# A graph-transformer network on one core: zero fill, weight loads, weight products and two row sums put in other places

## The chip, the cores and the metric

The kernel runs on one core of a Trainium2 chip. The metric is the device time of one execution in microseconds (us). The core has five engines with a queue of instructions each: PE (TensorE, matrix products), DVE (VectorE), ACT (ScalarE), POOL (GpSimd) and SP (SyncE, which here only issues DMAs). DMAs are issued by SP, ACT and POOL, and are carried out by 16 shared DMA engines.

## The reference, cut to what matters

There are 1250 nodes with 512 channels and 40000 edges with 8 attributes. Two layers follow each other; the change lies in the first.

```python
xn = layernorm(x)
x = x + L0_gnn(xn, edges, edge_attr) + L0_mix(xn)   # both from the same xn
x = x + L0_ffn(layernorm(x))
xn = layernorm(x)
x = x + L1_gnn(xn, edges) + L1_mix(xn)
x = x + L1_ffn(layernorm(x))

def L0_gnn(x, ...):                  # graph transformer
    z = layernorm(x, g, b)
    q, k, v = z @ Wq.T + bq, z @ Wk.T + bk, z @ Wv.T + bv     # 8 heads of 64
    s = (q[src] . k[dst]) / 8 + att_bias                      # per edge and head
    agg = segment_softmax(s, src) summed over v[dst]
    x = x + agg @ Wo.T + bo
    h = silu(layernorm(x, g2, b2) @ W1.T + b1)
    return x + h @ W2.T + b2

def L0_mix(x, ...):                  # linear attention and a small feed-forward
    qp, kp = relu(x @ Wq + bq) + 1e-3, relu(x @ Wk + bk) + 1e-3
    v = x @ Wv + bv
    a = (qp @ (kp.T @ v)) / (qp @ sum(kp))                    # per head
    h = layernorm(a @ Wo + bo + x)
    return layernorm(relu(h @ W1 + b1) @ W2 + b2 + h)

def L1_gnn(x, ...):                  # graph convolution: normalised sums, then two weights
    return (aggregate(x @ W_gcn) + b_gcn) @ W_dense + b_dense
```

## The kernel before, in words

The nodes are padded to 1280, ten tiles of 128. The graph attention is done densely: a DRAM table `adj` of 1280 x 1280 x 9 numbers (eight attribute sums and a count for each pair of nodes, 59 MB) is filled with zeros, the edges are added into it by indirect DMAs, and later each tile of 128 nodes reads its slab of the table.

**Zero fill (lines 219 to 228).** `zrow` is a row of zeros in SBUF, cleared by POOL. Four DMAs of 14.4 MB each, and a small one, write it over `adj`, all issued on SP.

**Edge preparation (to line 293).** From source, target and attributes the kernel makes a key for each edge. Keys are transposed and stored to `key_d` in three DMAs (line 269, on ACT). The weights `wgt` go through an exponential (283) and are split into three bf16 parts in `w3`: three casts and two subtractions on DVE.

**The edge generator `scatter_edges` (line 302 on).** It runs over the 313 columns of 128 edges in batches of three, 105 batches. `load_keys` (311) reads a broadcast row `kr` of keys back from `key_d`. DVE compares keys (`eq` 325, `eqx` 335), TensorE sums the weights of equal keys (317), DVE makes `tot` (342) and `idx` (348), and POOL issues one indirect scatter-add into `adj` for each column (351). `tot` and `idx` have 48 buffers. A scatter waits for those of the batch two before it. A call `pump(n)` in the other code draws n batches from the generator.

**Weight products (`weight_products`, line 402 on).** A second generator multiplies pairs of weights that the later layers need as products: it loads them in halves of 256 columns (`fw`), transposes, multiplies (`product`) and stores to DRAM. It is drawn between the tiles of the mix's attention.

**Stage A (to 799 us).** Under the pool `mix`: x is loaded in ten DMAs on ACT into `xn`, then the weights `wk`, `wv` and the bias rows `mixrows` (lines 456 to 458 by their helpers 129 and 123, on ACT too). Layer norm and transposes for each tile, K and V for each tile (`kp`, `va`, evicted by DVE), the product `kv`, Q, the attention tiles with their layer norm, then the two layers of the mix's feed-forward; its last loop, the f-stage (line 565 on), also adds x and stores to `xm_d`. Under the pool `gqkv` come the graph's layer norm (`z`, line 157), its transposes into `zT` (174), `xb = xn + bo` (stored to `xb_d`), K and Q in column chunks (`kT`, evicted by DVE at 599; `qs` by ACT, stored to `q_d`), V for each tile, and last the gcn fold (lines 613 to 635): `W_gcn @ W_dense` to `wgd_d`, the bias rows to `bsum_d`, and `fold_q`. TensorE's matmuls of all this are recorded at the helper's line 179.

**Slab stage (799 to 1190 us).** `load_tile` (652, 656) loads a slab of `adj` and a tile of `q_d`; the load waits for all scatters.

**The wo stage and the feed-forward (from line 849).** `fetch` loads a tile of the attention's output and of `xb`. Per tile: output projection, sum `X = mm + xb` (884), layer norm (833 to 845), `z` on ACT (889), transposes (897), `zT` (901, 904), and the first feed-forward layer. This loop's order is written out by hand. In the second part the layer's output and `xm` are added to X (921, 922).

**What sets the order.** Except where written by hand, a scheduler chooses the order on each engine when the kernel is built, from modelled times; each engine then runs its queue in order. The DMAs of SP and ACT share eight semaphores, dealt in turn: a DMA which gets a semaphore that an earlier DMA still holds waits on its engine until that one has landed.

Of the kernel before, what the change touches and what calls it, by code (L numbers as in the profile page):

```python
# [22 lines left out]
P = 128  # L23
# [43 lines left out]
def tile_gps_layers(ctx: ExitStack, tc: tile.TileContext, a, out):  # L67
# [13 lines left out]
    def ps_tr(shape=(P, 512), name="tr"):  # L81
        return psum.tile(list(shape), F32, tag="tr", bufs=2, name=name)

# [43 lines left out]
    def load_w(pool, name, kc, n, tag="w", bufs=None, eng=nc.sync):  # L127
        t = pool.tile([P, kc, n], F32, tag=tag, name=name, bufs=bufs)
        eng.dma_start(t, a[name].rearrange("(c p) o -> p c o", p=P))
        return t  # L130
# [65 lines left out]
    adj = dram.tile([NROW, CH], F32, name="adj")  # L196
    key_d = dram.tile([EC, P], F32, name="key_d")
    cnt_d = dram.tile([NP, NP], F32, name="cnt_d")
    q_d = dram.tile([P, KC, NP], F32, name="q_d")
    xm_d = dram.tile([NP, C], F32, name="xm_d")  # L200
    xb_d = dram.tile([NP, C], F32, name="xb_d")
    att_d = dram.tile([P, KC, NP], F32, name="att_d")
    deg_d = dram.tile([P, NP], F32, name="deg_d")
    w1f_d = dram.tile([NEXP, P, KC, 256], F32, name="w1f_d")
    wgd_d = dram.tile([P, KC, C], F32, name="wgd_d")
    wqd_d = dram.tile([P, KC, NKEYS], F32, name="wqd_d")
    bsum_d = dram.tile([P, C], F32, name="bsum_d")

    s_xn = ctx.enter_context(ExitStack())
    pxn = s_xn.enter_context(tc.tile_pool(name="xn", bufs=1, side="right"))
    xn = pxn.tile([P, NT, C], F32, tag="xn", name="xn")

    s_edge = ctx.enter_context(ExitStack())
    pe = s_edge.enter_context(tc.tile_pool(name="edge", bufs=1, side="right"))
    s_tmp = ctx.enter_context(ExitStack())
    ptmp = s_tmp.enter_context(tc.tile_pool(name="edgetmp", bufs=1, side="right"))

    zrow = pe.tile([P, 1800], F32, name="zrow")
    nc.gpsimd.memset(zrow, 0.0)
    adj_p = adj[0:NKEY, :].rearrange("(p r) c -> p (r c)", p=P)
    step = 16 * 1800
    for z0 in range(0, NKEY * CH // P, step):
        nc.sync.dma_start(adj_p[:, z0:z0 + step].rearrange("p (a f) -> p a f", f=1800),
                            zrow[:, None, :].to_broadcast([P, 16, 1800]))
    nc.sync.dma_start(adj[NKEY:NROW, :].rearrange("(p r) c -> p (r c)", p=P), zrow[:, :(G + 1) * CH])
# [74 lines left out]
    def scatter_edges():  # L303
# [3 lines left out]
        def load_keys(c0):  # L307
            cn = min(G + B, EC - c0)
            kr = pew.tile([P, (G + B) * P], F32, name="kr")
            queue = nc.scalar if c0 == 0 else nc.sync  # L310
            queue.dma_start(kr[:, :cn * P],
                            bass.AP(tensor=key_d.tensor, offset=key_d.offset + c0 * P, ap=[[0, P], [1, cn * P]]))
            return kr
# [26 lines left out]
        def scatter(acc, cnt, c0, g, place):  # L340
            tot = pew.tile([P, B, CH], F32, name="tot", bufs=48)
            nc.vector.tensor_reduce(tot[:, :g], acc[:, :g].rearrange("p c (t n) -> p c n t", t=3),
                                    axis=AX.X, op=OP.add)
            row = pew.tile([P, B], F32, name="row")
            nc.vector.scalar_tensor_tensor(row[:, :g], cnt[:, :g], 1.0, keyrel[:, c0:c0 + g],
                                           op0=OP.is_equal, op1=OP.mult)
            idx = pew.tile([P, B], I32, name="idx", bufs=48)
            nc.vector.tensor_tensor(idx[:, :g], row[:, :g], spare[:, place:place + g], op=OP.add)
            near, cur = (scattered[-1] if scattered else []), []
            for c in range(g):  # L350
                st = nc.gpsimd.indirect_dma_start(  # L351
                    out=adj, out_offset=bass.IndirectOffsetOnAxis(ap=idx[:, c:c + 1], axis=0),
                    in_=tot[:, c, :], in_offset=None, compute_op=OP.add)
                for x in cur + near:
                    tc.declare_no_dep(st.ins, x.ins, reason="rows of a batch and of the one next to it differ")
                for x in (scattered[-2] if len(scattered) > 1 else []):
                    tc.add_manual_dep(st.ins, x.ins.name, SYNC, reason="rows of batches may agree")
                cur.append(st)
            scattered.append(cur)
# [40 lines left out]
    def weight_products(pool):  # L400


        def turned(name):
            wT = pool.tile([P, KC, C], F32, tag="fwT", name=name + "T")
            for k in range(KC):
                if k % 2 == 0:
                    w = pool.tile([P, KC, 256], F32, tag="fw", name="fw", bufs=2)
                    nc.sync.dma_start(w, a[name].rearrange("(c p) o -> p c o", p=P)[:, :, k * P:(k + 2) * P])
                ps = ps_tr((P, KC, P))
                for c in range(KC):  # L410
                    nc.tensor.transpose(ps[:, c, :], w[:, c, k % 2 * P:(k % 2 + 1) * P], ident)
                nc.scalar.copy(wT[:, k, :].rearrange("p (c q) -> p c q", c=KC), ps)
            return wT

# [29 lines left out]

    with (tc.tile_pool(name="mix", bufs=1) as pm, tc.tile_pool(name="mixw", bufs=2) as pw,
# [6 lines left out]
        wk = load_w(pm, "L0_mix_Wk", KC, C, bufs=2, eng=nc.scalar)  # L454
        wv = load_w(pm, "L0_mix_Wv", KC, C, bufs=2, eng=nc.scalar)
        rows = rows_bc(pm, a["mix_rows"], len(MIX_ROWS), name="mixrows", eng=nc.scalar)
# [5 lines left out]

        def load_x(t):
            x_t = pw.tile([P, C], F32, tag="x_t", name="x_t")
            if t == NT - 1:
                nc.vector.memset(x_t, 0.0)
                nc.sync.dma_start(x_t[:TAIL], a["x"][t * P:N, :])
            else:
                nc.sync.dma_start(x_t, a["x"][t * P:(t + 1) * P, :])
            return x_t  # L470
# [85 lines left out]
        for t in range(NT):  # L556
            x_t = load_x(t)
# [6 lines left out]
            nc.vector.tensor_tensor(f, f, x_t, op=OP.add)  # L564
# [17 lines left out]
    with tc.tile_pool(name="gqkv", bufs=2) as pq:  # L582
        gbv = rows_bc(pq, a["gnn_rows"][0:2], 2, name="gbv")
# [4 lines left out]
        for t in range(NT):  # L588
            z = pq.tile([P, C], F32, tag="z", name="z")
            norm(pq, z, xn[:, t, :], 1e-5, "lnz")  # L590
            transposed(zT, z, t, "att_g", "att_b")
            xb = pq.tile([P, C], F32, tag="xb", name="xb")
            nc.vector.tensor_tensor(xb, xn[:, t, :], gbv[:, 1, :], op=OP.add)
            nc.scalar.dma_start(xb_d[t * P:(t + 1) * P, :], xb)
        for c0, cn in CHUNKS:
            for m in range(KC):
                ps = ps_mm()
                chan_mm(ps[:, :cn], wk, m, zT, c0, cn)
                nc.vector.tensor_scalar(kT[:, m, c0:c0 + cn], ps[:, :cn], col("gnn_bk", m), None, op0=OP.add)
# [11 lines left out]


        brow = rows_bc(pq, a["l1_rows"], len(L1_ROWS), name="l1rows")
        wg = load_w(pq, "gcn_WgT", KC, C, bufs=3)
        wd = load_w(pq, "L1_gnn_W_dense", KC, C, bufs=3)
        wqn = load_w(pq, "l1_Wq", KC, C, bufs=3)
        for m in range(KC):
            ps = ps_mm()
            mm(ps, [(wg[:, c, m * P:(m + 1) * P], wd[:, c, :]) for c in range(KC)])
            qs = pq.tile([P, 512], F32, tag="qs", name="qs", bufs=3)  # L620
            nc.scalar.copy(qs, ps)
            nc.sync.dma_start(wgd_d[:, m, :], qs)
            pump(1)
        ps = ps_mm()
        mm(ps, [(col("gcn_b", c).to_broadcast([P, P]), wd[:, c, :]) for c in range(KC)])
        qs = pq.tile([P, 512], F32, tag="qs", name="qs", bufs=3)
        nc.vector.tensor_tensor(qs, ps, brow[:, 0, :], op=OP.add)
        nc.vector.tensor_tensor(qs, qs, brow[:, 1, :], op=OP.add)
        nc.sync.dma_start(bsum_d, qs)
        bd = pq.tile([P, KC, H], F32, name="bd")  # L630
        nc.vector.tensor_tensor(bd, own_head, col("l1_wq", 0, 4)[:, :, None].to_broadcast([P, KC, H]), op=OP.mult)
        ps = ps_tr((P, KC, H))
        for m in range(KC):
            mm(ps[:, m, :], [(wqn[:, c, m * P:(m + 1) * P], bd[:, c, :]) for c in range(KC)])
        nc.scalar.copy(fold_q[:, :, :H], ps)
# [212 lines left out]
    with tc.tile_pool(name="gff", bufs=1) as pf, tc.tile_pool(name="gffw", bufs=2) as pw:  # L848

        zT = pf.tile([P, KC, NP], F32, name="zT2")  # L850
        wo = load_w(pf, "gnn_WoT", KC, C)
        inputs, zs = {}, {}
# [8 lines left out]
        def fetch_xm(t):  # L861
            inputs[t] = pw.tile([P, C], F32, tag="xm", name="xm")
            nc.sync.dma_start(inputs[t], xm_d[t * P:(t + 1) * P, :])
# [14 lines left out]
        with tc.manual_schedule(engines={nc.tensor.engine, nc.vector.engine, nc.scalar.engine}):  # L878
            for t in range(NT + 2):
                if t < NT:  # L880
# [3 lines left out]
                    nc.vector.tensor_tensor(X[:, t, :], ps, xb, op=OP.add)  # L884
                    if t + 5 < NT:
                        fetch(t + 5)
# [25 lines left out]
            for c, (c0, cn) in enumerate(CHUNKS):  # L912
                n = cn // P
                for k, t in enumerate(range(c0 // P, c0 // P + n)):
# [7 lines left out]
                    nc.vector.tensor_tensor(X[:, t, :], X[:, t, :], inputs.pop(t), op=OP.add)  # L922
# [1063 lines left out]
```

## Time and profile before

| what | us |
|---|---|
| median of 3 runs | 2408.09 (2406.57 to 2413.21) |
| the profiled execution | 2412.46 |
| its span on the core | 2410.7 |
| last packet of the zero fill | 174.09 |
| slab stage begins, ends | 798.67, 1190 |
| feed-forward's second part ends | 1381 |

Mean TensorE clock granted over the span: 0.913 of full speed. Busy time by stretch, from the trace, in us (columns: stretch, its length, PE, its weight loads, DVE, ACT and POOL with the number of instructions, granted clock, share of the DMA engines, GB/s):

```profile
50.00:80.00 30.00, 0.00 (x0) 0.00 (x0) 13.96 (x7) 5.15 (x5) 0.00 (x0) 1.00 1.02 421
80.00:175.00 95.00, 72.39 (x219) 34.86 (x220) 36.21 (x141) 6.55 (x18) 0.00 (x0) 1.00 1.01 412
520.00:640.00 120.00, 57.51 (x380) 27.88 (x379) 119.52 (x512) 2.43 (x12) 101.11 (x63) 0.60 0.54 111
690.00:772.00 82.00, 80.69 (x369) 42.44 (x368) 47.64 (x207) 5.33 (x9) 68.90 (x44) 1.00 0.46 79
772.00:799.00 27.00, 26.60 (x85) 14.03 (x83) 2.77 (x4) 2.53 (x5) 0.17 (x1) 0.97 0.27 88
```

How to read the rows of the other views. A row of the timeline has start and duration in us, engine, line, operation, output and inputs by the program's names, a count, and in brackets how long the engine idled before it and what released it. Engines with a q are their instruction queues, where DMAs are issued. The chain of waits lists, in order of time, the piece of work that each step waited for. A row of the slices has 40 digits, each the busy share of a fortieth of the span (60 us) in tenths.

### The profile page before, as it was taken

The numbers are of one execution on the slowest core, as the hardware profiler recorded it, in microseconds if no ns is written. First come the engines' busy times: TensorE is split into PE (matmuls) and PEld (weight loads), VectorE is DVE, ScalarE is ACT, GpSimd is POOL, SyncE is SP. The second block draws the span as 40 slices with busy tenths as digits, with TensorE's granted clock in tenths as the row PEclk, the third lists the DMA queues.
The fourth block names the chain that finished last, engine by engine and source line by source line (L and its number), as shares of the span: only waits on it lengthen the run. The fifth ranks groups of instructions, "written<-read, shape, count | busy, mean of one in ns | idle before, by whom it ended". The sixth has DMA issues, their size and how long they took to land.

```text
span 2410.7 us, 29628 instructions
## 1 busy us (share of the span) xinstructions
PE 1986.3 (82%) x10548; PEld 1172.5 (49%) x10548; DVE 1531.4 (64%) x4886; ACT 782.1 (32%) x1465; POOL 695.6 (29%) x448
## 2 busy tenths in 40 slices
PE   0299698675399699999799999999999999978943
PEld 0147465442145366666544545667445446555521
DVE  3528858789892398999550446655222242599997
ACT  0101011010000276676441156665111122244653
POOL 2008888888886000000000000000000000036665
PEclk9999798786599799999999999999899999989975
DMA  9997564345644655655250100000400102000000
GB/s 393 423 367 179 102 130 66 42 70 114 158 95 73 244 193 208 240 195 209 79 175 14 40 19 1 1 1 20 145 26 27 35 3 68 22 22 9 10 9 17
DMA packets 132593, 255.79 MB, mean 106 GB/s; under 512 B 51678, under 2 KB 87191, under 8 KB 130781
## 3 DMA queue, kind: packets, MB, share of 16 engines
q1 hardware_dynamic: 80576, 234.11, 26.5%
q0 software_dynamic: 46512, 8.02, 7.3%
q10 hardware_dynamic: 5356, 11.77, 1.3%
q8 instruction: 83, 1.36, 0.2%
q14 instruction: 66, 0.53, 0.1%
HBM read 161.05 MB, written 92.80 MB: 105 GB/s over the span
## 4 chain that ended last, share of the span: by engine, by line
PE 60%; DVE 22%; DMA 7%; ACT 6%; issue 2%; POOL 1%; ACTq 0%; SPq 0%; DVEq 0%; POOLq 0%
PE mm L179 33%; PE sc L678 4%; PE one L727 4%; DVE eqx L335 4%; ACT wT L718 3%; DVE eq L325 3%; PE one L717 2%; PE ag L1370 2%; PE sc L1049 2%; PE av L1103 2%; PE one L1090 2%; DMA adj<-zrow 2%; DVE sc L1730 2%; DMA mixrows<-in_mix_rows 2%; DMA adj<-tot,idx 1%
## 5 line engine op out<-in xcount | busy, mean ns | idle before, releaser
L351 POOL DMA_INDIRECT adj<-tot,idx x313 | 498.8, 1594 | 259.5 <-DMA kr<-key_d 162.0
L707 DVE SCALAR_TENSOR_TENSOR ex<-ex,slab 128x1280 f32<-128x1280 f32 x80 | 197.2, 2506 | 0.0
L1301 DVE SCALAR_TENSOR_TENSOR X<-mm,gate,X 128x512 f32<-128x512 f32 x80 | 60.1, 751 | 199.5 <-PE mm L179 199.4
L335 DVE TENSOR_SCALAR_CACHE_REDUCE eqx<-kr,key 128x384 bf16<-128x384 f32 (+1 forms) x312 | 175.5, 600 | 1.6 <-PE even L317 1.2
L325 DVE SCALAR_TENSOR_TENSOR eq<-kr,key,upto 128x128 bf16<-128x128 f32 (+2 forms) x313 | 146.1, 476 | 17.4 <-PE even L317 14.2
L1239 POOL MEMSET padded<- 128x128 f32 x3 | 0.5, 205 | 539.6 <-DVE faT L1124 539.6
L718 ACT COPY wT<-one 128x512 f32<-128x512 f32 (+1 forms) x240 | 115.9, 517 | 93.8 <-PE one L717 89.3
L717 PE MATMUL one<-ident,ex 128*128 128x128 f32 x800 | 126.0, 286 | 24.1 <-ACT wT L718 20.3
L179 PE MATMUL mm<-w,hT 128*128 128x512 f32 (+1 forms) x320 | 145.8, 608 | 0.0
L179 PE MATMUL mm<-faT,w 128*128 128x512 f32 (+1 forms) x384 | 138.6, 514 | 0.7 <-ACT bs L1123 0.7
L688 DVE CUSTOM_DVE_ANT_0 ex<-sc,none 128x1280 f32<-128x1280 f32 x80 | 115.7, 1485 | 14.8 <-PE sc L678 13.7
L678 PE MATMUL sc<-kT,q 64*128 64x512 f32 (+1 forms) x480 | 104.3, 558 | 21.9 <-DMA q<-q_d 18.6
L717 PEld LDWEIGHTS one<-ident,ex 128*128 128x128 f32 x800 | 84.6, 141 | 67.0 <-ACT wT L718 48.3
L1063 DVE CUSTOM_DVE_ANT_0 ex<-sc,cmask 128x512 f32<-128x512 f32 (+3 forms) x144 | 72.9, 560 | 69.2 <-PE sc L1049 69.1
L664 POOL DMA_DIRECT2D deg_d<-cnt x10 | 8.5, 846 | 362.1 <-ACT attT L734 315.8
L700 ACT ACTIVATE ex<-ex,low 128x1280 f32<-128x1280 f32 x80 | 104.7, 1361 | 10.8 <-DVE low L693 10.8
L179 PEld LDWEIGHTS mm<-faT,w 128*128 128x128 f32 x384 | 72.8, 190 | 66.0 <-issue 65.0
L727 PE MATMUL one<-wT,gva 128*64 128x128 f32 x1600 | 101.3, 284 | 3.7 <-ACT wT L718 2.1
L317 PEld LDWEIGHTS <-eq 128*128 128x128 bf16 x625 | 43.0, 102 | 120.2 <-DVE eq L325 79.4
L1295 ACT ACTIVATE hT<-mm,cols 128x512 f32<-128x512 f32 (+1 forms) x48 | 29.0, 608 | 217.1 <-PE mm L179 217.0
L179 PEld LDWEIGHTS mm<-w,hT 128*128 128x128 f32 (+1 forms) x320 | 61.6, 193 | 76.7 <-issue 76.7
L727 PEld LDWEIGHTS one<-wT,gva 128*64 128x64 f32 x1600 | 91.6, 143 | 13.6 <-ACT wT L718 13.6
(493 smaller groups left out, 4100.9 us busy)
## 6 DMA issues: line engine op xcount, KB each, us to landing
adj<-zrow SPq DMA_DIRECT2D x4, 14400.0 KB
slab<-adj SPq DMA_DIRECT2D x10, 5760.0 KB
kr<-key_d SPq DMA_DIRECT2D x50, 576.0 KB
cnt_d<-cnt SPq DMA_DIRECT2D x10, 640.0 KB
deg_d<-cnt POOLq DMA_DIRECT2D x10, 640.0 KB
adjT<-cnt_d SPq DMA_DIRECT2D x5, 1280.0 KB
adj<-tot,idx POOLq DMA_INDIRECT x313
fw<-in_L_ffn_W SPq DMA_DIRECT2D x8, 512.0 KB
```

The source lines that it names most:

```text
L179: nc.tensor.matmul(ps, lhsT=l, rhs=r, start=i == 0, stop=i == len(pairs) - 1)
L325: nc.vector.scalar_tensor_tensor(eq[:, :n], kr[:, k0 * P:k0 * P + n], key[:, c0 + c:c0 + c + 1], upto[:, B - 1 - c:, :].rearrange("p c x - ...
L335: nc.vector.tensor_scalar(eq[:, :n * P], kr[:, k0 * P:(k0 + n) * P], key[:, c0 + c:c0 + c + 1], None, op0=OP.is_equal, op1=OP.add, accum_o ...
L351: st = nc.gpsimd.indirect_dma_start(out=adj, out_offset=bass.IndirectOffsetOnAxis(ap=idx[:, c:c + 1], axis=0), in_=tot[:, c, :], in_offset ...
L678: nc.tensor.matmul(sc[e][:, d0:d0 + dn], lhsT=q[half(e), m, :], rhs=kT[half(e), m, d0:d0 + dn], start=True, stop=True)
L688: nc.vector.tensor_tensor_reduce(out=ex, in0=sc[e][:, :NP], in1=none, scale=-0.125, scalar=-LOWEST, op0=OP.add, op1=OP.min, accum_out=low[ ...
L700: nc.scalar.activation(exs[e], exs[e], AF.Exp, bias=low[:, e:e + 1], scale=-1.0)
L707: nc.vector.scalar_tensor_tensor(exs[e], exs[e], 1.0, sl[:, :, hd], op0=OP.mult, op1=OP.mult, accum_out=den[:, hd:hd + 1])
L717: nc.tensor.transpose(ps[:, k, :], weights[t, m][e][:, (d0 + k) * P:(d0 + k + 1) * P], ident)
L718: nc.scalar.copy(wT[:, d0:d0 + dn, :], ps[:, :dn])
L727: nc.tensor.matmul(av[half(e), 0, :], lhsT=va[:, d, hd * D:(hd + 1) * D], rhs=turned[e][:, d, :], start=d == 0, stop=d == NT - 1)
L1063: nc.vector.tensor_tensor_reduce(out=exs[e][:, d0:d0 + dn], in0=sc[k][e][:, :dn], in1=cmask[:, NP - n + d0:NP - n + d0 + dn], scale=-0.125 ...
```

## The change

- `zrow` is cleared by DVE, as the first work, and the five fill DMAs are issued at the top of the program; nothing about their sizes changes.
- The mix's `wk`, `wv` and `mixrows` are loaded on SP instead of ACT, and wait for all five fill DMAs. The second kr load goes on ACT like the first.
- `tot` and `idx` get 32 buffers instead of 48.
- The gcn fold becomes part of `weight_products`, in halves of 256 columns.
- In the graph's projections, the layer norm's apply, the transposes' evictions and kT's evictions are done by ACT.
- The sum with `bo` goes from before `xb_d` to the wo stage; the sum with x from the f-stage to the second part of the feed-forward, where x is loaded beside `xm`. `xb_d` now gets xn itself.

```diff
+    zrow = pe.tile([P, 1800], F32, name="zrow")
+    nc.vector.memset(zrow, 0.0)
+    fill = [nc.sync.dma_start(adj_p[:, z0:z0 + step].rearrange("p (a f) -> p a f", f=1800),
+                              zrow[:, None, :].to_broadcast([P, 16, 1800]))
+            for z0 in range(0, NKEY * CH // P, step)]
+    fill.append(nc.sync.dma_start(adj[NKEY:NROW, :].rearrange("(p r) c -> p (r c)", p=P), zrow[:, :(G + 1) * CH]))
...
-    nc.gpsimd.memset(zrow, 0.0)
...
-            queue = nc.scalar if c0 == 0 else nc.sync
+            queue = nc.scalar if c0 < 2 * G else nc.sync
...
-            tot = pew.tile([P, B, CH], F32, name="tot", bufs=48)
+            tot = pew.tile([P, B, CH], F32, name="tot", bufs=32)
...
+        wT = fetched("gcn_WgT")
+        for x in range(2):
+            o = slice(x * 256, (x + 1) * 256)
+            w = half_of("L1_gnn_W_dense", x)
+            for m in range(KC):
+                product(wT, w, m, wgd_d[:, m, o])
+                if m % 2:
+                    yield
...
+            ps = ps_mm((P, 256))
+            mm(ps, [(col("gcn_b", c).to_broadcast([P, P]), w[:, c, :]) for c in range(KC)])
+            f = pool.tile([P, 256], F32, tag="fs", name="fs", bufs=2)
+            nc.vector.tensor_tensor(f, ps, fb[:, 0, :], op=OP.add)
+            nc.vector.tensor_tensor(f, f, fb[:, 1, :], op=OP.add)
+            nc.sync.dma_start(bsum_d[:, o], f)
+        wT = fetched("l1_Wq")
...
+        late = [nc.sync.dma_start(wk, a["L0_mix_Wk"].rearrange("(c p) o -> p c o", p=P)),
+                nc.sync.dma_start(wv, a["L0_mix_Wv"].rearrange("(c p) o -> p c o", p=P)),
+                nc.sync.dma_start(rows, bass.AP(tensor=a["mix_rows"].tensor, offset=a["mix_rows"].offset,
+                                                ap=[[0, P], [C, len(MIX_ROWS)], [1, C]]))]
+        for ld in late:
+            for x in fill:
+                tc.add_manual_dep(ld.ins, x.ins.name, SYNC, reason="the zeros go first")
...
-            nc.vector.tensor_tensor(f, f, x_t, op=OP.add)
...
-            norm(pq, z, xn[:, t, :], 1e-5, "lnz")
-            transposed(zT, z, t, "att_g", "att_b")
-            nc.vector.tensor_tensor(xb, xn[:, t, :], gbv[:, 1, :], op=OP.add)
-            nc.scalar.dma_start(xb_d[t * P:(t + 1) * P, :], xb)
+            nc.scalar.activation(z, xn[:, t, :], AF.Identity, scale=r, bias=b)
...
+                nc.scalar.activation(zT[:, c, t * P:(t + 1) * P], ps[:, c, :], AF.Identity,
+                                     scale=col("att_g", c), bias=col("att_b", c))
+            nc.scalar.dma_start(xb_d[t * P:(t + 1) * P, :], xn[:, t, :])
...
-                nc.vector.tensor_scalar(kT[:, m, c0:c0 + cn], ps[:, :cn], col("gnn_bk", m), None, op0=OP.add)
+                nc.scalar.activation(kT[:, m, c0:c0 + cn], ps[:, :cn], AF.Identity, bias=col("gnn_bk", m))
...
+        bo = rows_bc(pf, a["gnn_rows"][1:2], 1, name="gbo")[:, 0, :]
...
+                    nc.vector.tensor_tensor(X[:, t, :], X[:, t, :], bo, op=OP.add)
...
-                    nc.vector.tensor_tensor(X[:, t, :], X[:, t, :], inputs.pop(t), op=OP.add)
+                    xm = inputs.pop(t)
+                    for k2 in range(2):
+                        nc.vector.tensor_tensor(X[:, t, :], X[:, t, :], xm[:, k2, :], op=OP.add)
```

## The prediction

> **What bounds the kernel now.** The change touches everything up to 799 us (edge preparation, linear attention, projections) and the 48 us after 1190; what lies behind is the same code. I read the slices of the page first, for who is busy when.
>
> ```profile
> DVE  3528858789892398999550446655222242599997
> POOL 2008888888886000000000000000000000036665
> DMA  9997564345644655655250100000400102000000
> ...
> L351 POOL DMA_INDIRECT adj<-tot,idx x313 | 498.8, 1594 | 259.5 <-DMA kr<-key_d 162.0
> ```
>
> One digit is 60 us. POOL, which does nothing here but the 313 scatter-adds of line 351, idles for three slices while the DMA engines are full, then keeps one digit for ten slices. Next the timeline of POOL and the issue rows (start, duration in us), for what opens and what closes that run.
>
> ```profile
> 175.86 1.78 POOL L351 DMA_INDIRECT adj<-tot,idx  x1 [162.03 <-DMA kr<-key_d]
> 177.94 1.55 POOL L351 DMA_INDIRECT adj<-tot,idx  x1 [0.30 <-issue]
> ...
> 691.74 1.55 POOL L351 DMA_INDIRECT adj<-tot,idx  x1 [0.30 <-DVE eq L325]
> ...
> 770.62 1.55 POOL L351 DMA_INDIRECT adj<-tot,idx  x1 [0.30 <-issue]
> ...
> 10.94 105.36 SPq L226 DMA_DIRECT2D adj<-zrow  x4
> 116.33 35.63 SPq L228 DMA_DIRECT2D adj<-zrow  x1
> 54.40 0.50 ACTq L269 DMA_DIRECT2D key_d<-kt  x1
> 75.88 0.34 ACTq L311 DMA_DIRECT2D kr<-key_d  x1
> ```
>
> The zero fill's last packet ends at 174.09 in the trace's DMA records and the first scatter starts 1.8 us later: the fill opens the run, not the keys that the bracket names. From there a scatter starts every 1.85 us; 313 of them need 579 us and took 596.5. Last, the chain of waits (start, duration).
>
> ```profile
> 10.94 43.38 DMA adj<-zrow
> 54.40 0.50 ACTq L269
> ...
> 732.56 61.96 PE mm L179 x168
> 794.51 4.10 PE tr L179 x32
> 798.67 0.32 SPq L652
> 799.04 17.35 DMA q<-q_d
> ...
> 1222.79 0.69 DVE X L884
> 1223.50 0.70 DVE lnfst L833
> ...
> 1226.13 0.81 ACT z L889
> 1226.94 0.35 ACT zT L901
> 1227.35 0.29 issue
> 1227.64 0.69 DVE X L884
> ```
>
> The scatters landed at about 773.7 (last start plus 3), yet the slab loads that wait for them are issued at 798.67: TensorE's K, Q, V and gcn fold end last, so the stage holds a tail of 25 us. After it the same slab stage runs to 1190. In the wo stage a tile takes 4.85 us (1222.79 to 1227.64), a serial DVE chain.
>
> **The fill.** zrow is cleared by DVE first of all, so fill 1 is issued at about 2.5 instead of 10.94, first packet near 5 (before: 2.8 us from issue to packet). If all five fills followed each other, all would be over some 8 us earlier. They don't. In the changed kernel's build the eight DMA semaphores are dealt in another order, and a DMA whose semaphore is taken waits, on its issuing engine, for the earlier one to land: the fifth x load on ACT's queue waits for fill 1, and fill 2 on SP for the first kr load. The trace of before shows this kind of wait: the third key_d store at 54.40 begins 1.5 us after fill 1's last packet (52.88), and kr goes out only at 75.88. There it cost nothing, fills 2 to 4 being in the ring. Now they stand behind it:
> - fill 1 lands: 14.75 MB at 418 GB/s (DMA records, 40 to 160 us) is 35.3 us, with 2.8 MB of loads alternating about 7, landing 1.5: 5 + 44 = 49.
> - from there, as 54.40 to 75.88 before and with xn loads ahead: key and x issues 3.5, two table loads 2.6, exp 2.3, five w3 casts on DVE at 2.77 (13.9) and copies 1.2, kr issue: 72.8. It lands 3.3 to 4.5 later, 76.5; fill 2's first packet 79.5.
> - 44.25 MB of fill and 2.7 MB of kr and xb beside it: 46.9 / 0.418 = 112 us, so 191.8. First scatter 193.6: **17.7 later** than before.
>
> A rule speaks about this place. The Trainium skill, "DMA: Bandwidth & Descriptors", section "Anatomy of one DMA — SWDGE (gpsimd) path", says that DMA engines do not wait on semaphores; the issuing sequencer waits before dispatch. By it everything behind fill 2 on SP stands too, and the 27 us between 50 and 79 are nearly empty, which is what I sum. If only the order of landing were tied, the fill would end at 5 + 141 (59 MB) + 22 of other traffic = 168, 6 us earlier than before. No row of before shows a fill held in SP's queue, so I keep both ends: −8 and +21; I take +17.7, since the chain of semaphores is in the build and each link has a duration.
>
> **The mix weights** (wk, wv, mixrows) move from 56.65–67 on ACT to SP behind the fill: issued at 193.6, the rows usable at about 208 instead of 99.93; K and V start near 200 instead of 104. The same page, "Rules for kernel authors", says to issue a DMA early and wait late; by it 96 us of delay would show. By the rows it doesn't, as long as POOL has edges: POOL needs its sixth batch of edges at 193.6 + 5 × 5.55 = 221, and five are prepared in the waiting time. What counts is DVE's lead over POOL. Before, the idx of batch 63 was ready at 509.6 and scattered at 534.65: lead 25; at batch 90 it was 682.8 against 691.74: 8.9. Counting DVE's changed order (kp and va at 1.6 to 1.8 a tile, 3.6 a batch): batch 20 is ready 27 us later than before, batch 33 35.5 later (eight TensorE groups of Wq and fw, 13.8, on which DVE's qpT waits), the folds in the attention tiles add 0 to 9. POOL is 17.7 later, less the 1.7 it lost early for lack of edges, 16. So the lead at 63 is 25 + 16 − (35.5 to 44.5) = +5.5 to −3.5. I take no loss there, narrowly.
>
> **Evictions.** In the LNz section ACT takes z (0.53 on DVE), four zT (0.34 each) per tile and eight 0.74 and four shorter kT; the xb sum (0.66) and the f-stage's x sum (0.73) go: 10 × (0.53 + 1.36 + 0.66) + 8 = 33 of DVE and 10 × 0.7 later. ACT, 3.7 busy of 50 us at 640 to 690, has room. It lifts the lead at batch 90, and the path gains nothing of it where POOL is the bound; if DVE bound, those 40 us would be gained at most.
>
> **The fold of gcn** (20 matmuls of 512 columns, about 9 us, with waits for weights, two sums, five stores) goes from 779–798.7 to the attention tiles of the mix, as 40 halves. TensorE's K, Q, V then end at about 770 even with DVE 38 later at the f-stage's end. So POOL is last: 193.6 + (770.62 − 175.86) − 1.7 = 786.5, landed 789.6, slab issued 789.7: **−9.0** against 798.67. kr on ACT for a second load, and 32 tot/idx buffers for 48, cost nothing: the lead never passed 65 us, 12 batches.
>
> **The two sums.** The bo sum is another 128x512 on the serial wo chain: 0.69 plus 0.03 gap, on 8 tiles before the first FF matmuls, +5.8; its broadcast row load ahead of the first xb load 0.7: **+6.5**. Bounds: 0 if DVE waited for TensorE (it waits for matmuls twice in ten), 7.9 if all ten count. The x sum beside the second FF layer, 10 × 0.72, and its doubled loads lie under a TensorE that is 139.9 busy of 141 us: 0, at most 0.7 at the last tile.
>
> Sum: −9.0 + 6.5 = −2.5. Profiled run 2412.46 (span 2410.7 + 1.8) gives about 2410; the median of before lies 4.4 under its profiled run, so 2408.09 − 2.5 = **2405.6**; a measurement tells about 0.3%, 7 us, from no change.
>
> **Rivals.**
> - A, as summed (0.5): 2398 to 2414. The first scatter may fall at 189 to 197, the wo chain cost 0 to 8.
> - B, POOL starves at batches 60 to 66 because K/V started 96 us later (0.3). Price: each us of DVE's slip past 41 (25 + 16) at batch 63 is a us of the end; from 51 on the kernel is slower by more than 0.3%. For it: DVE is 119.5 busy of 120 at 520 to 640 and can't catch up; I count up to 44.5, and waits for fw loads in the fold are not in it. Against it: the removed sums. At a slip of 55, 2420; at 62, 2427.
> - C, the change does what it says: fill uninterrupted, over at 168, first scatter 170, slab stage at 767 to 775, TensorE then last or level: −24 to −32 + 6.5, so 2383 to 2391 (0.13). Against it: the semaphore order above.
> - D, as A but the hole is half as long, since x loads fill it and kr comes sooner (0.07): 2392 to 2398.
>
> Chances: faster by over 0.3% (under 2400.9) is C, D and a bit of A, 0.22; slower (over 2415.3) most of B, 0.28; the rest 0.50. Range 2389 to 2426.
>
> **What would show it.** Fill 2 issued near 77 and a hole in the GB/s slices at 50 to 80; first scatter near 194; first K matmul near 200; leads at batches 63 and 90; the slab issue near 790, released by the scatters and not by TensorE; X of line 884's successor every 5.57 us. I am wrong if fill 2 goes out before 60 (C), or if POOL's gaps between 450 and 650 name DVE and add up to over 5 us (B).

## The result, and the profile after

The changed kernel takes 2431.49 us (median of 4 runs, 2429.49 to 2435.22) against 2410.65 before (4 runs): ratio 1.0088, interval 1.0076 to 1.0100. It is slower by about 21 us, where 2405.6 was predicted and 2426 was the upper end. The profiled execution spans 2427.7 us, 17.0 more than before. Four marks in both traces say where they lie (us):

| stretch | before | after | difference | predicted |
|---|---|---|---|---|
| start to the first slab issue | 798.7 | 812.0 | +13.3 | -9.0 |
| slab stage, to the last store of the attention | 391.7 | 390.7 | -1.0 | 0 |
| wo stage, to the first FF matmul | 48.1 | 54.4 | +6.3 | +6.5 |
| FF, to the last tile's sum `X = mm + X` | 141.8 | 141.8 | 0 | 0 |
| the rest | 1030.4 | 1028.8 | -1.6 | 0 |

One line of the sum is wrong, by 22 us: the first stage. (The last tile's added x sum, 0.7, falls in the rest.) The slices of the page after:

```profile
DVE  4605945878975299999661455666222132599998
POOL 1006888887888200000000000000000000036665
DMA  8796655544454646655260110000410102000000
```

POOL again keeps one digit, but a slice later at both ends. The beginning of the stage, first by the timeline's rows of ACT, SP and POOL, then by the waits of SP's queue up to 100 us (us in total, times, longest), then by the windows (columns as in the stretches of before):

```profile
75.39 0.33 ACTq L312 DMA_DIRECT2D kr<-key_d  x1
...
79.34 21.43 SPq L109 DMA_DIRECT2D adj<-zrow  x2
...
194.50 1.78 POOL L352 DMA_INDIRECT adj<-tot,idx  x1 [182.39 <-DMA kr<-key_d]
```

```profile
SPq L109 <- DMA kr<-key_d: 76.2, 1, 76.2
```

```profile
50.00:80.00 30.00, 3.91 (x16) 3.16 (x17) 23.36 (x57) 7.25 (x10) 0.00 (x0) 1.00 0.32 110
```

Fill 2 is issued at 79.34; it has stood in SP's queue for 76.2 us, and the wait names the kr load. From 50 to 80 the DMA engines move 110 GB/s instead of 421: the hole is there. (Each of the four large fill DMAs is 14.75 MB, 128 x 28800 numbers of 4 bytes, and not 14.4.) The fill's last packet ends at 192.4 (191.8 predicted), the first scatter starts at 194.5 (193.6). The middle went wrong. TensorE and DVE at the mix's Q, from the timeline:

```profile
318.02 3.60 PE L209 MATMUL mm<-xnT,L_mix_Wq 128*128 128x512 f32 x8
321.46 3.62 PE L209 MATMUL mm<-fw,L_ffn_WoT 128*128 128x256 f32 x16
324.91 3.60 PE L209 MATMUL mm<-xnT,L_mix_Wq 128*128 128x512 f32 x8
328.34 3.62 PE L209 MATMUL mm<-fw,L_ffn_WoT 128*128 128x256 f32 x16
...
321.66 0.75 DVE L548 TENSOR_SCALAR qpT<-mm,bqe 128x512 f32<-128x512 f32 x1 [2.83 <-PE mm L209]
328.55 0.75 DVE L548 TENSOR_SCALAR qpT<-mm,bqe 128x512 f32<-128x512 f32 x1 [6.14 <-PE mm L209]
```

```profile
318.00:346.00 28.00, 28.00 (x113) 18.58 (x111) 4.03 (x10) 3.16 (x9) 23.43 (x16) 1.00 0.53 79
```

Eight groups, Wq and fw in turn, follow each other until 345.6 without a matmul of the edges between them, and each takes 3.44 us (318.02 to 321.46). DVE, which has the results of Wq to fetch, stands still for 2.83 in front of the first qpT and for 6.14 in front of each of the next three; of these 28 us (the row of the windows) it works 4. A Wq group of four products of 512 columns is recorded as eight matmuls that start 0.43 apart. Now the stage's end: the first K matmul and V's last eviction before (timeline of PE and DVE), the chain of waits after with the slab issue that follows (timeline of SP), and the timeline of POOL where it lost most.

```profile
656.36 4.53 PE L179 MATMUL mm<-zT,gnn_WkT 128*128 128x512 f32 x5 [0.51 <-DVE zT L174]
777.38 0.69 DVE L609 TENSOR_TENSOR gva<-mm,gbv 128x512 f32<-128x512 f32 x1 [2.74 <-PE mm L179]
```

```profile
694.85 6.15 PE mm L209 x10
...
766.40 44.80 PE mm L209 x128
811.23 0.70 DVE gva L647
812.36 17.01 DMA q<-q_d
```

```profile
811.99 0.32 SPq L665 DMA_DIRECT2D slab<-adj  x1
```

```profile
559.57 1.67 POOL L352 DMA_INDIRECT adj<-tot,idx  x1 [6.79 <-DVE tot L343]
...
565.24 1.54 POOL L352 DMA_INDIRECT adj<-tot,idx  x1 [0.30 <-DVE idx L349]
...
802.63 1.54 POOL L352 DMA_INDIRECT adj<-tot,idx  x1 [0.30 <-issue]
```

TensorE starts the graph's K at 694.8 (before: 656.4), and V's last eviction comes 116 us later, at 811.2 (before: 121 us later, at 777.4); TensorE is busy for 115.6 of the 117 us. POOL starved at batch 62 (6.79 us for DVE), and its last scatter started at 802.6 where 786.5 was summed. Two ends, both late. A slab load is issued about 3 us after the last scatter's start, so POOL alone would have let it go at about 805.7: TensorE's end is the later by 6 us. The wo stage's chain, with a second sum per tile:

```profile
1239.21 0.69 DVE X L902
1239.92 0.70 DVE X L903
1240.65 0.71 DVE lnfst L846
...
1243.27 0.81 ACT z L908
1244.08 0.35 ACT zT L920
1244.49 0.29 issue
1244.79 0.69 DVE X L902
```

A tile takes 5.58 us where it took 4.85.

### The profile page after: what moved, and what is told of

It is laid out like the page before. It is cut to its first block, busy times and chain, and to the rows that moved or that the text cites. A ratio compares the mean times of both kernels' runs of the same rounds, so it can differ in the third digit from the quotient of the medians.

```text
span 2427.7 us, 29796 instructions
## 1 busy us (share of the span) xinstructions
PE 1970.3 (81%) x10588; PEld 1177.6 (49%) x10588; DVE 1513.5 (62%) x4841; ACT 809.3 (33%) x1528; POOL 695.2 (29%) x447
## 4 chain that ended last, share of the span: by engine, by line
PE 58%; DVE 21%; ACT 6%; issue 2%; DMA 1%; POOL 0%; DVEq 0%; SPq 0%; ACTq 0%; POOLq 0%
PE mm L209 31%; PE sc L691 4%; PE one L740 4%; DVE eqx L336 3%; ACT wT L731 3%; PE one L730 3%; PE ag L1391 2%; DVE eq L326 2%; PE sc L1070 2%; PE av L1124 2%; PE one L1111 2%; DVE sc L1751 2%; DVE ix L1692 1%; DVE ix L1701 1%; DVE rest L1704 1%
## 5 line engine op out<-in xcount | busy, mean ns | idle before, releaser
L701 DVE CUSTOM_DVE_ANT_0 ex<-sc,none 128x1280 f32<-128x1280 f32 x80 | 115.5, 1481 | 13.2 <-PE sc L691 11.9
L730 PEld LDWEIGHTS one<-ident,ex 128*128 128x128 f32 x800 | 86.1, 143 | 67.3 <-ACT wT L731 47.9
L318 PE MATMUL even<-w,eq 128*128 128x27 bf16 x313 | 23.7, 183 | 112.2 <-DVE eq L326 107.9
```

What stands on the lines that cost most here:

```text
L701: nc.vector.tensor_tensor_reduce(out=ex, in0=sc[e][:, :NP], in1=none, scale=-0.125, scalar=-LOWEST, op0=OP.add, op1=OP.min, accum_out=low[ ...
L730: nc.tensor.transpose(ps[:, k, :], weights[t, m][e][:, (d0 + k) * P:(d0 + k + 1) * P], ident)
```

## The experiments

Theory M: what costs is the mix starting 90 us later (first kp eviction 209.0 instead of 118.7), because TensorE and DVE then reach the graph's K, Q, V late, with little slack left. Rival F: what costs is the scatters' late start behind the hole. Times below are medians with the ratio to the kernel before on the same chip; "slab" is the first slab issue of the profiled execution, "V over" the start of V's last eviction, "lead" the time from a batch's idx on DVE to its first scatter on POOL.

**e1, weights early.**

```diff
-        late = [nc.sync.dma_start(wk, ...), nc.sync.dma_start(wv, ...), nc.sync.dma_start(rows, ...)]
-        for ld in late:
-            for x in fill:
-                tc.add_manual_dep(ld.ins, x.ins.name, SYNC, reason="the zeros go first")
+        nc.scalar.dma_start(wk, ...); nc.scalar.dma_start(wv, ...); nc.scalar.dma_start(rows, ...)
```

> The changed kernel, but the mix's wk, wv and mixrows go back on ACT's queue behind the x loads and no longer wait for the fill; the fill stays as in the changed kernel, with its hole. Theory M (the time is lost because the mix's K and V begin 100 us late, TensorE's K, Q, V of the graph then end last): first K matmul near 100, first scatter 190 to 198 as now, DVE's lead at batch 63 back above 25 us, slab stage begins at about 792 (194.5 + 595 + 3), 20 us earlier than 812; time about 2411. Rival F (the fill's hole, that is the scatters' late start, is what costs): the start of the scatters is unchanged, so the time stays above 2425.

2407.01 us, ratio 0.9982 (0.9975 to 0.9990); slab 788.2. First scatter 191.4, first kp 89.8, lead at batch 63 31.6, V over at 767.8. The end is now the scatters': the last starts at 785.09, the slab load 3.1 later (timeline of POOL and SP).

```profile
785.09 1.55 POOL L352 DMA_INDIRECT adj<-tot,idx  x1 [0.30 <-issue]
...
788.21 0.32 SPq L662 DMA_DIRECT2D slab<-adj  x1
```

The scatters start as late as in the changed kernel, and 24 us are back: theory M, and F alone falls. What F is worth shows in that POOL is now last.

**e2, the fill issued by POOL; e3, the same with the weights early.**

```diff
-    fill = [nc.sync.dma_start(adj_p[:, z0:z0 + step]...
+    fill = [nc.gpsimd.dma_start(adj_p[:, z0:z0 + step]...
```

> The changed kernel with its five fill DMAs issued by POOL instead of SP, so that they hold no semaphore of the shared eight and wait for no kr; the mix's weights still wait for the fill. Theory M and rival F both: no hole at 50 to 79, fill over at 166 to 172, K and V of the mix from about 176 instead of 200, slab stage 20 to 25 us earlier (787 to 792), time 2406 to 2412. A third theory (the hole costs nothing because the loads behind it are what the first batches wait for): fill earlier but time within 5 us of 2431. If DMAs issued by POOL move their bytes more slowly, the fill ends after 192 and the time is above 2431.

2431.64 us, 1.0084 (1.0061 to 1.0107); slab 811.7. The hole closed and the fill was over at 165.9, but nothing was gained. In the rebuilt order of ACT's queue the first kr load comes last of all, behind copies that wait for TensorE. ACT's and POOL's timeline:

```profile
190.95 0.81 ACTq L312 DMA_DIRECT2D kr<-key_d  x2
...
200.28 1.71 POOL L352 DMA_INDIRECT adj<-tot,idx  x1 [180.86 <-DVE eq L326]
```

The mix's first kp came 18 us earlier (190.8), but the first four batches of edges, which DVE had prepared at 86 to 99 in the changed kernel, now came at 198 to 209, behind the fill; the f-stage began at 575, as before the edit (576). The expectation failed, and the run doesn't tell what a hole costs.

> Both edits: the fill issued by POOL without its hole, and the mix's weights early on ACT. Theory M: first scatter near 174, K and V near 105, TensorE and POOL end level at 772 to 782, slab stage 30 to 38 us before the changed kernel's 812; with the wo chain's 6.3 us still in it 2393 to 2401. Rival F: as the fill alone gives, 2406 to 2412, the weights adding nothing.

2405.95 us, 0.9978 (0.9971 to 0.9985); slab 786.0, first scatter 185.7. Below the changed kernel by what e1 gave; my 2393 to 2401 was too hopeful: up to the fill's end, now at 183.7, 16.5 MB of other transfers moved beside it instead of the 8.7 of e2. The early loads, 4.2 MB, are about half of the difference.

**e4, the gcn fold alone moved** (before, with the fold's lines taken from behind V into the weight products, as in the diff of the change).

> The kernel before with one part of the change alone: the gcn fold moved from behind V into the weight products beside the mix's attention. If the fold's 21 us were a tail on TensorE and the attention tiles have room (TensorE 113 busy of 148 us there): slab stage begins 14 to 20 us before 798.7, time 2389 to 2396. Rival (the work is only moved, TensorE is the bound of the whole stage and arrives at K, Q, V later by as much): within 4 us of before.

2394.11 us, 0.9927 (0.9904 to 0.9950); slab 781.6, 17.1 earlier. The fold was nearly a pure tail: the stage lost the 20.5 us that lay behind V's last eviction, and V itself came 3.5 later (780.9 for 777.4), which is what the fold costs beside the attention tiles. The lead at batch 63 went from 25.0 to 22.7. V's last eviction now ends the stage (timeline of DVE and SP):

```profile
780.86 0.69 DVE L642 TENSOR_TENSOR gva<-mm,gbv 128x512 f32<-128x512 f32 x1 [2.74 <-PE mm L179]
...
781.62 0.32 SPq L660 DMA_DIRECT2D slab<-adj  x1
```

**e5, the late weights alone** (before, with wk, wv and mixrows waiting for the fill).

> The kernel before with one part alone: wk, wv and mixrows on SP, waiting for the fill. Theory M: fill over at 170 to 175 as before, K and V of the mix from 185 to 190 instead of 104 to 119, first K of the graph 30 to 38 us later (662 to about 697), then V and the gcn fold behind it: slab stage begins at 828 to 838 instead of 798.7, time 2438 to 2450. Rival F (the start of the scatters decides): first scatter unchanged at 176, so within 5 us of before.

2436.82 us, 1.0117 (1.0095 to 1.0138); slab 820.7. The scatters started earlier than before (165.3, since the weights no longer compete with the fill), and the stage still ended 22 us later: theory M a second time, and rival F wrong in sign. The size is below my 30 to 38 in part because the fill was over at 163.7, 6 to 11 us before the time that I had assumed; the first K came at 678.5, where I had 697, and the rest of that difference stays open. The chain of waits:

```profile
759.96 56.25 PE mm L179 x142
816.21 4.45 PE tr L179 x32
```

It is the tail of before, moved: V until 799.1, then the fold (the last 4.45 are its `fold_q`).

**e6, the fill's place alone** (before, with zrow cleared by DVE and the fill at the top).

> The kernel before with one part alone: zrow cleared by DVE first and the fill issued at the top. Here fill 2 is tied to the first key_d store, so the hole should be 5 to 10 us, not 27; the weights still come early on ACT. First scatter 170 to 180, since the hole takes back what the early start gives; TensorE's tail (V and gcn fold) sets the end as before: time 2403 to 2413. Rival F (fill position decides): the time moves by as much as the first scatter does.

2414.27 us, 1.0018 (1.0010 to 1.0027); slab 799.6, first scatter 178.1. Issued 8 us earlier, the fill ends 2 us later. In this build too fill 2 waits, until 55.9, and no packet of the fill moves for 9.7 us after the first: that part of the change brings nothing by itself, and if anything costs a little.

**e7, both sums back** in the changed kernel.

> The changed kernel with the two sums where they were (bo ahead of xb_d, x in the f-stage). The wo stage should lose its 6.3 us (a tile 4.85 instead of 5.58). Theory M: DVE is full from the f-stage to the graph's layer norm, so TensorE's K starts 5 to 14 us later and its V ends as much later, slab stage at 817 to 826: time 2430 to 2439, the move of the sums was worth 0 to 8 us. Rival (the sums in stage A lie beside the scatters and cost nothing): time 2425.

2417.00 us, 1.0021 (1.0013 to 1.0029): 14 us below the changed kernel, against both expectations; slab 809.3. The wo stage was back at 48.1. But the edit did a second thing: without the early xb_d stores on ACT the semaphores were dealt otherwise, the hole closed, and the fill was over at 166.6. From the f-stage's start to V's end the stage took 255 us (553.5 to 808.5), against 235 in the changed kernel: the two sums go with 20 us there, more than the 14 of their own instructions. The two effects had to be taken apart (e12, e13).

**e8, the evictions alone** on ACT in the kernel before.

> The kernel before with one part alone: the graph's layer norm apply, transposes' and kT's evictions on ACT. Between 638 and 662 DVE is what K waits for, and TensorE has no pause afterwards, so K starts 8 to 18 us earlier and V and fold end as much earlier, with the scatters' landing at 774 as the floor: slab stage 781 to 791, time 2394 to 2405. Rival (TensorE waits for ACT instead, or K's start is set elsewhere): within 4 us of before.

2413.25 us, 1.0008 (0.9999 to 1.0017); slab 797.4. No gain, as the rival said. DVE had room for more edges (lead at batch 90 33.3 instead of 8.9), but the first K began at 658.3, and before at 656.4; TensorE has no long pause from there. Its timeline:

```profile
658.28 2.08 PE L179 MATMUL mm<-zT,gnn_WkT 128*128 128x512 f32 x2
```

**e9 and e10, the parts that pay:** fold and x sum (with its ten loads) moved, bo sum left; in e10 with the evictions.

```diff
-            nc.vector.tensor_tensor(f, f, x_t, op=OP.add)
...
+                    xm = inputs.pop(t)
+                    for k2 in range(2):
+                        nc.vector.tensor_tensor(X[:, t, :], X[:, t, :], xm[:, k2, :], op=OP.add)
```

> The kernel before with two parts: the gcn fold moved as in the fold-only run, and the x sum moved from the f-stage into the feed-forward's second part (the bo sum stays ahead of xb_d). In the fold-only run TensorE's V ended last, at 780.9, the scatters at 774. The x sum's 10 x 0.73 lie on a full DVE ahead of K, Q, V, so V ends at 771 to 775 and the scatters take over: slab stage at 774 to 776, time 2386 to 2390. Rival (the x sum in the f-stage was hidden): slab stage stays at 781, 2394.

2387.91 us, 0.9914 (0.9891 to 0.9937); slab 774.3, V over at 770.6, the scatters last. V came 10 us earlier than in e4; the stage gained 7.3 of it, because the scatters then end last.

> As the run before it, with the projections' evictions on ACT too. With the scatters last, at 774, nothing is left to gain: slab stage at 774 to 776, V well before that, time 2385 to 2390, within 3 us of the run before it. Rival (evictions shorten the path): 5 us or more below it.

2385.81 us, 0.9892 (0.9876 to 0.9909); slab 773.6, V over at 764.2. This is the fastest kernel of the study, about 25 us below before and 46 below the changed one; between e9 and e10 the intervals don't decide. FF took 141.8 in both: the x sum there is free but for the last tile's 0.7.

**e11, is TensorE alone late?** The changed kernel, which here leaves out three quarters of V's products.

```diff
-            node_mm(ps, zT, t, wv)
+            mm(ps, [(zT[:, 0, t * P:(t + 1) * P], wv[:, 0, :])])
```

> The changed kernel with three quarters of V's matmuls in the graph's projections left out (only the first 128 of 512 channels are summed, so V is wrong). If TensorE alone sets the end, V ends 26 us earlier, at 785, and so does the stage: 2406. If POOL starved just as far (last scatter at 802.6, landed 3.1 later), the slab stage is issued at 805 to 807 instead of 812, released by the scatters: 2424 to 2427.

2425.88 us, 1.0067 (1.0048 to 1.0087); slab 804.7, 3.0 after the last scatter's start (timeline of DVE, POOL and SP).

```profile
785.50 0.69 DVE L647 TENSOR_TENSOR gva<-mm,gbv 128x512 f32<-128x512 f32 x1 [0.17 <-PE mm L209]
...
801.63 1.54 POOL L352 DMA_INDIRECT adj<-tot,idx  x1 [0.30 <-issue]
804.66 0.32 SPq L665 DMA_DIRECT2D slab<-adj  x1
```

V's end came 26 us earlier and the stage's end 7: POOL's late end stood right behind TensorE's.

**e12, weights early and bo back; e13, bo back alone.** Both leave the early xb_d stores out; e12 has e1's edit too.

```diff
-            nc.scalar.dma_start(xb_d[t * P:(t + 1) * P, :], xn[:, t, :])
+            nc.vector.tensor_tensor(xb, xn[:, t, :], gbv[:, 1, :], op=OP.add)
+            nc.scalar.dma_start(xb_d[t * P:(t + 1) * P, :], xb)
...
-                    nc.vector.tensor_tensor(X[:, t, :], X[:, t, :], bo, op=OP.add)
```

> The changed kernel with two parts undone: the mix's weights early on ACT, and the bo sum ahead of xb_d, so that the early xb_d stores go too. In this build fill 2 is tied to the second key_d store instead of the first kr load. Theory (the early stores made the hole by shifting the deal of semaphores): hole 5 to 10 us, first scatter 175 to 180, slab stage set by the scatters at 774 to 779, wo stage 48 us as before: time 2386 to 2392. Rival (the hole comes with the fill's place at the top): first scatter above 188, time above 2398.

2391.65 us, 0.9920 (0.9899 to 0.9940); slab 777.0, first scatter 179.2, wo stage 48.5. Fill 2 goes out at 55.73, and the window of 50 to 80 is full again (391 GB/s):

```profile
50.00:80.00 30.00, 0.00 (x0) 0.00 (x0) 14.34 (x9) 5.15 (x5) 0.00 (x0) 1.00 1.01 391
```

The fill still stands at the top, and no packet of it moves for 9.6 us instead of 33.4. So the long hole doesn't come with the fill's place. In e1, which differs from e12 by the bo sum and its early stores alone, it lasted 28.8: the early stores made it.

> The changed kernel with the bo sum alone put back ahead of xb_d; the mix's weights still wait for the fill. Without the early xb_d stores fill 2 is tied to the sixth x load instead of the first kr load, so the hole should close: fill over at 163 to 168, first scatter 168 to 171, K and V of the mix at 183. If hole and late weights add up (the weights wait for the fill's end, so each us of hole is a us of delay for the mix): f-stage 20 to 24 us earlier than 576, V's end and slab stage at 788 to 797 instead of 812, wo stage 6.3 shorter: time 2405 to 2414. Rival (the hole mattered little, as in the run with both sums back, where the slab stage came only 2.7 earlier): slab stage at 806 to 810, time 2420 to 2425.

2408.32 us, 0.9991 (0.9981 to 1.0001); slab 800.1, first scatter 168.1, f-stage at 556.5, V over at 799.3. As the first theory said, but for a slab issue 3 us later than my range; fill 2 now waits for an x load and goes out at 54.57. The step from e13 to the changed kernel is the slab issue (800.1 to 812.0, 12 us) and the wo stage (47.9 to 54.4, 6.5 us): 18.4, which is what the spans differ by (2409.3 and 2427.7). Within the 12, two things are mixed. The f-stage begins 20 us later (556.5 to 576.3), with the weights that wait for the fill's end, and then 8 of them come back before V's end (242.8 us from there to V's end in e13, 234.9 in the changed kernel), as the bo sum is off DVE. No run has the lighter DVE without the hole, so the split is read from these marks and not measured by itself. The step from e12 to e13 is the late weights alone: V ends 37 us later, of which the stage shows 23.1, because in e12 the scatters ended last.

The slab issue of the changed kernel can now be followed from run to run:

| run | what it adds to the run above | slab | step | ends last |
|---|---|---|---|---|
| before | | 798.7 | | TensorE, the fold |
| e4 | fold moved | 781.6 | -17.1 | TensorE, V |
| e9 | x sum moved | 774.3 | -7.3 | scatters |
| e10 | evictions on ACT | 773.6 | -0.7 | scatters |
| e12 | fill at the top, second kr load on ACT, 32 buffers | 777.0 | +3.4 | scatters |
| e13 | mix's weights behind the fill | 800.1 | +23.1 | TensorE, V |
| changed | bo sum moved: hole, and less on DVE | 812.0 | +11.9 | TensorE, V |

Each step is one profiled execution against another, and executions of one kernel spread by 3 to 12 us in time, so the 0.7 and the 3.4 are no findings. In another order the steps would be others, since two ends compete: the x sum is worth 9.2 between e13 and e7 (800.1 and 809.3). The second kr load and the 32 buffers were not run alone; in e12, which has both, the scatters run for 594.6 us, and before for 594.8.

## Why the prediction was wrong

Two steps failed, TensorE's end and DVE's slip, and either alone would have put the slab issue past 805 instead of 789.7. ("Slip" is how much later than before a batch is ready.)

- **The fill** was right, 191.8 for 192.4, each step within 3 us: kr issued at 72.8 forecast and 75.4 measured, the hole in the fill's packets from 49 to 79.5 forecast and from 48.1 to 81.5 measured, and the rest 112 forecast and 111 measured. One reading was wrong: "No row of before shows a fill held in SP's queue." SP's waits of before show it twice, without a hole, since the fill before was still moving:

```profile
SPq L226 <- DMA xn<-in_x: 33.3, 2, 30.6
SPq L226 <- DMA key_d<-kt: 22.0, 1, 22.0
```

- **"TensorE's K, Q, V then end at about 770 even with DVE 38 later"**: this is the step that failed and set the end. K did start 38.5 later (694.8 for 656.4), but V was over at 811.2, so the slab loads were released by TensorE and not by POOL. From the first K to 770 would be 75 us. It took 116.4, and the trace of before had 121.0 for the same stretch: laid on the later start, that would have put TensorE last, at about 815. The prediction shows no working for its 770. Half the true price per group, as in the next step, could account for it: K, Q and V are 26 groups at 3.44 and 8 shorter ones, some 100 us by this estimate, and half of that is missing.
- **The mix weights**: this step failed too. "So the lead at 63 is 25 + 16 − (35.5 to 44.5) = +5.5 to −3.5. I take no loss there, narrowly." DVE's slip at batch 33 was 52.2 us (356.4 against 304.2), not 35.5, and 52.7 at batch 63 (562.3 against 509.6). The mis-sized term is the "eight TensorE groups of Wq and fw, 13.8": they took 27.6, since a group is eight recorded matmuls of 0.43 and not four. The start was 3 late as well (batch 20 by 30.1 for 27); 3.1 and 13.8 add to 16.9, for the 16.7 that were missing. The folds, for which I had kept 0 to 9, added 0.5. That the weights' place makes it is shown: from batch 21 to batch 33 the slip grew by 21.0, and by 19.4 with the late weights alone (e5); with them early in the changed kernel (e1) the lead at 63 was 31.6 and V over at 767.8. Why the new order puts the eight groups in one block stays open.
- **The past-the-range part.** The marks account for 19.5 us of the miss in the profiled executions (22.3 in the first stage, less 2.8 elsewhere). The other 6.4 of the 25.9 are a matter of which executions were profiled: I put the median 4.4 under the profiled run, as before, and after it lay 2.0 above.
- **Rival B** had the mechanism, and its sign came true: POOL's gaps between 450 and 650 name DVE and add up to 9.3. Its price was low. A slip of 52.7 made 2417 by its rule; POOL's gaps in all are 14.0 and its end was 16 later than summed, and with V out of the way (e11) the kernel takes 2425.9. What B lacked was the second end: TensorE, 6 us behind POOL.
- **Rival C** did not come true, and would not have paid as I priced it. In e13 the fill was over at 166.3 and the first scatter started at 168.1, as C has it, but the weights still waited, TensorE ended last, and the slab loads went out at 800.1 instead of 767 to 775.
- **The fold**: its tail was worth 17.1 (e4), summed as part of the 25 us tail; right, because the tail was read from the trace. Its matmuls, given as "about 9 us", are the same half price: 20 matmuls are five groups of 3.44, 17.2. **The evictions**: no gain on the path, right (e8). **The two sums**: +6.3 in the wo stage and 0 in the feed-forward, right; but the x sum taken from the f-stage is worth 7.3 of the stage's end where TensorE is last (e9), and I counted nothing on the path. The early xb_d stores were counted as bytes only; that they make the hole, and so belong to the price of the bo sum's move, I did not see.
- Of the two rules of the Trainium skill ("DMA: Bandwidth & Descriptors"), that of "Rules for kernel authors" to issue a DMA early speaks of a fixed setup cost that overlaps; that 96 us would show by it was my reading. It was right in sign: between e12 and e13 the mix's first kp comes 77 us later, and 23 of these reach the slab issue. The other ("Anatomy of one DMA — SWDGE (gpsimd) path"), that a wait for a semaphore is taken on the issuing sequencer before dispatch, agrees with the trace: fill 2 stands in SP's queue until 79.34 and the fill ends at 192.4, where a tie of the landings alone would have given 168.

## What to carry to other kernels

Before a start is moved later, follow every engine of the moved stage to its end and price it from the length that the trace shows for the same loop, not from a count of instructions; two resources can be late at once, and lifting one shows the other. A change of several parts should be run in its parts: here the fold and the x sum gain 24 us, the late weights lose 23 and the bo sum's move 18 (12 by the slab issue, 6.5 in the wo stage), and the whole looked like one small loss. Where DMAs share a few semaphores dealt in turn, an added early store can tie a large transfer to an unrelated load, so read the waits of the new build after each edit.

## What the runs showed of the hardware

The fill ran at the same speed from POOL's queue as from SP's: between 120 and 160 us, where almost nothing else moved, it was 286 to 293 packets of 7200 B in 5 us (413 to 422 GB/s by the trace's DMA records) from SP in before, and 289 to 293 (416 to 422) from POOL in e2. With loads in 2048-B packets beside it, the two queues' packets went nearly one for one: 235 of 7200 B and 215 of 2048 B from 50 to 55 us in e2, 234 and 205 from 30 to 35 us in before. In these windows the share went by packets and not by bytes. The granted TensorE clock was 0.54 of full speed from 576 to 694 in the changed kernel, where TensorE is busy for 60.6 of 118 us, and 0.98 from 694 to 811, where it is busy for 115.6 of 117. This makes no rule by itself: from 50 to 80, with TensorE busy for 3.9 of 30 us, the record says 1.00.
